# A graph layer on one core: float32 rows and sums in place of three bfloat16 parts, in-degrees per group of chunks, layernorm on whole pieces, no row loads

## The chip, the core and the metric

The kernel runs on one core of a Trainium2 chip. The metric is the device time of one execution in microseconds, lower being better. A core has five engines that work side by side and wait for one another by semaphores: PE (TensorE, matrix products into PSUM), DVE (VectorE, elementwise work and reductions), ACT (ScalarE, functions and copies), POOL (GpSimd, which here does nothing but issue the indirect DMAs that gather rows), and SP (SyncE, which issues plain DMAs). SBUF is the on-chip memory of 128 partitions; the table of node features is in DRAM.

## The reference

12,500 nodes with 128 features each, 200,000 edges sorted by destination, hidden width 512.

```python
h = relu(layernorm(x))                        # rows of 128, eps 1e-5
agg = segment_sum(h[src], dst, 12500)         # sum of h over a node's in-edges
deg = segment_sum(ones, dst, 12500)
agg = agg / maximum(deg, 1)
y = relu(agg @ Wg + h @ Ws + bg)              # 128 -> 128
y = tanh(y @ W1 + b1)                         # 128 -> 512
y = tanh(y @ W2 + b2)                         # 512 -> 512
out = x + y @ W3 + b3                         # 512 -> 128
```

All of it is float32.

## The kernel before

*Chunks.* The edges are cut into 1563 chunks of 128. Since the edges are sorted, the destinations of chunk c lie close to node 8c; each chunk has a window of 144 nodes around that place (88 or 56 for the last ones). A chunk is summed with a matrix product: the gathered rows, one edge on each partition, are the weights, and a 0/1 matrix `oh` (edge by window node, one where the edge's destination is that node) is the moving operand. The result, features by nodes, is added into the PSUM tile `agg` of the block to which the window's nodes belong. A block is 512 nodes (the last blocks are 256, three times 128 and 84; 28 blocks in all), so some 64 chunks belong to one; a window that lies across two blocks' border is done in two halves. A second product with a matrix of ones as weights adds the columns of `oh` into the PSUM tile `deg`: the in-degrees. Both are in `add(c)`; the call on PE itself is line 292.

*Rows in three parts.* `htab` in DRAM holds h as three bfloat16 numbers whose sum is the float32 number, 768 bytes a row (`split`, lines 175 to 178). So a chunk takes three bfloat16 products for `agg` and one for `deg`.

*Where rows come from.* Three kinds of chunks: 96 "raw" ones (12 groups of 8, one group in every 40 chunks from chunk 256 on) gather rows of x itself at the start (line 133), while h is still being made, and are normalized on their own later (`raw_parts`); 17 "slow" ones, one in every 80, have their 128 rows loaded one by one by SP (`row_loads`: SP reads an index into a register, line 323, and issues a DMA of one row, line 298); the other 1450 are gathered by POOL with one indirect DMA each (`gather`, line 302) into one of 28 row buffers (`AHEAD`). A gather whose buffer is not free waits for the products of the chunk that held it. SP also loads `xb`, a block's rows of x, and stores the output.

*Setup.* x comes in pieces of 14 tiles of 128 nodes (the first in two, 4 and 10). For each tile DVE computes `bn_stats` and `bn_aggr` (lines 159 and 160), for each piece `factors` gives scale and shift, ACT normalizes tile by tile (line 170), ACT and DVE split, and SP writes the piece to `htab` (line 221). Then the destinations are turned into places in their windows (`dloc`, line 242) and tested against the windows' ends (`bad`, line 254); the test decides at the end whether a general path has to run, which does not happen with these inputs.

*Order.* All PE work is in program order. The loop over chunks makes the one-hot matrices of a group of 8 chunks one group ahead (`onehot`, line 345, on DVE), issues gathers up to 28 ahead, adds the chunk, and when a block's last chunk is in, queues that block's `layers`. These are a generator of some 14 parts, one of which is issued after every second chunk: the reciprocal `rd` of the in-degrees on DVE (lines 438 and 439), `mT` = agg times rd (441), then on PE the products with Ws and Wg (`pm`, ACT makes h0, line 449), W1 (h1, line 455), W2 (16 products of 512 columns, h2, line 464), W3 (16 products into `pt`), and on DVE the sum with x and b3 (`o`, lines 475 and 478). `own(s)` loads a block's x 40 chunks before the next block begins and lets ACT normalize it again into `hb`; `own_turned` transposes it 30 chunks later. From chunk 1376 (`QUICK`) on, the parts are placed by an estimate `there` of when a chunk's rows land.

Of the kernel before, what the change touches and what calls it, by code (L numbers as in the profile page):

```python
"""Pre-LN graph layer: x + MLP(relu(mean_agg(h) @ Wg + h @ Ws + bg)), h = relu(layernorm(x)).

Edges are taken 128 at a time. The rows h[src] of a chunk come by an indirect DMA, as three bfloat16
parts whose sum is exactly the float32 row. A chunk's destinations are compared with a fixed window
of nodes around those it would have if the sorted destinations were spread evenly; the rows times
that 0/1 matrix add the chunk's part of the sums, transposed, to PSUM, and a matrix of ones times it
the in-degrees. Some groups of chunks, gathered while h is still being made, take rows of x and are
normalized on their own. One chunk in many has its rows loaded one by one, by the sync engine, at
addresses read from its indices, beside the indirect DMAs of the others. When all chunks that reach
a block of nodes are done, its layers follow.  # L10

Whether every destination lies in its chunk's window is checked on the chip. If one does not, a
general path, for edges in any order, computes everything anew.
"""
# [7 lines left out]
F32 = mybir.dt.float32  # L22
BF16 = mybir.dt.bfloat16
# [6 lines left out]
P = 128  # L30
EPS = 1e-5
CPR = 16       # chunks of edges in a row of the index tiles
BLK = 512      # nodes in a block
PIECE = 14     # tiles of nodes in a piece of x
GRP = 8        # chunks of edges in a group
NRAW = 12      # groups that take rows of x
RAW0 = 256     # first chunk of the first of those
STEP = 40      # chunks from one of those to the next
AHEAD = 28     # chunks whose rows are loaded ahead
SLOW0 = 160    # first of the chunks whose rows are loaded one by one  # L40
EACH = 80      # gathers from one of those to the next
LOADS = 16     # rows whose indices are read together
QUICK = 1376   # from this chunk on, the layers go ahead as soon as they can
# First chunks and windows' widths: the spread of the destinations about even ones falls to the end.
WINDOWS = ((0, 144), (1496, 88), (1536, 56))
W_RAW = 160    # width in the groups that take rows of x
W_MAX = max(W_RAW, *(w for _, w in WINDOWS))

# In the general path:
NCOPY = 4      # tables of sums, and chunks of edges in a group  # L50
GPIECE = 16    # tiles of nodes in a piece of x
GAHEAD = 3     # groups of edges whose rows are loaded ahead


def windowed(ctx, tc, x, src, dst, Wg, Ws, bg, W1, b1, W2, b2, W3, b3, out, flag):
# [5 lines left out]
    NT = -(-N // P)            # tiles of 128 nodes: node = 128 * tile + partition  # L61
    NP = NT * P
    ROW = CPR * P              # edges in a row of the index tiles
# [7 lines left out]
    per = N * P // E           # nodes that a chunk spans when all are even  # L71
# [3 lines left out]
    # The raw groups are those that take rows of x; an edge of one lies anywhere in its group.  # L75
# [3 lines left out]
    # The slow chunks are those whose rows are loaded one by one, by the sync engine, which has  # L79
    # little else to do.  # L80
    slow, n = [], 0
    for c in range(SLOW0, NCH - 1):
        n -= not raw(c)
        if n < 0 and not raw(c):
            slow.append(c)
            n = EACH

    # A window lies around the nodes that its chunk spans when all are even.
# [18 lines left out]
    rows_one = ctx.enter_context(tc.tile_pool(name="rows_one", bufs=3))  # L107
# [8 lines left out]
    rsrc = const.tile([P, NRAW, GRP], I32, name="rsrc")  # L116
    rdst = const.tile([P, NRAW, GRP], I32, name="rdst")
    for t, a in ((rsrc, src), (rdst, dst)):
        a = a[RAW0 * P : RAW1 * P].rearrange("(u e) -> u e", u=NRAW)[:, : GRP * P]
        nc.sync.dma_start(t, a.rearrange("u (p k) -> p u k", p=P))  # L120
# [21 lines left out]
    nc.vector.memset(ones, 1.0)  # L142
    eps = const.tile([P, 1], F32, name="eps")
    nc.vector.memset(eps, EPS)
    lane = ps_c.tile([P, W_MAX], F32, name="lane")
    nc.vector.tensor_copy(lane, lane_i)

# [1 line left out]
    htab = dram.tile([NP, 3 * D], BF16, name="htab")  # L149
    scol = const.tile([P, NCOL], I32, name="scol")  # L150
    dloc = const.tile([P, NCOL], F32, name="dloc")
    norm_x = const.tile([P, 2, NT], F32, name="norm_x")
    norm_raw = const.tile([P, 2, NRAW * GRP], F32, name="norm_raw")
    mv_raw = const.tile([P, NRAW * GRP, 2], F32, name="mv_raw")

    def moments(pool, mv, xt, k):
        st = pool.tile([P, PIECE, 6], F32, name="st")
        for t in range(k):
            nc.vector.bn_stats(st[:, t, :], xt[:, t, :])
            nc.vector.bn_aggr(mv[:, t, :], st[:, t, :])  # L160

    def factors(norm, mv):
        rstd, shift = norm[:, 0], norm[:, 1]
        nc.scalar.activation(rstd, mv[:, :, 1], AF.Sqrt, bias=eps)
        nc.vector.reciprocal(rstd, rstd)
        nc.vector.scalar_tensor_tensor(shift, mv[:, :, 0], -1.0, rstd, op0=ALU.mult, op1=ALU.mult)

    def normalize(h, xt, k, norm):
        for t in range(k):
            nc.scalar.activation(  # L170
                h[:, t, :], xt[:, t, :], AF.Relu, bias=norm[:, 1, t : t + 1], scale=norm[:, 0, t : t + 1]
            )

    def split(parts, h):
        nc.scalar.copy(parts[:, :, 0, :], h)
        nc.vector.tensor_tensor(h, h, parts[:, :, 0, :], op=ALU.subtract)
        nc.scalar.copy(parts[:, :, 1, :], h)
        nc.vector.tensor_tensor(parts[:, :, 2, :], h, parts[:, :, 1, :], op=ALU.subtract)

    with tc.tile_pool(name="setup", bufs=1) as sp, tc.tile_pool(name="ln", bufs=2) as ln:  # L180

        def indices(name, a, col, pad):
# [9 lines left out]
            # Column r * CPR + q is chunk q of row r, with an edge on each partition.  # L192
# [7 lines left out]
        # The first piece in two, so that the work on it begins early.  # L200
        pieces = [(0, 4), (4, PIECE - 4)] + [(t, min(PIECE, NT - t)) for t in range(PIECE, NT, PIECE)]
        for i, (t0, k) in enumerate(pieces):
# [8 lines left out]
            if i == 1:  # L211
                indices("src", src, scol, 0)
            norm = norm_x[:, :, t0 : t0 + k]
            mv = ln.tile([P, PIECE, 2], F32, name="mv")
            moments(ln, mv, xt, k)
            factors(norm, mv[:, :k])
            h = ln.tile([P, PIECE, D], F32, name="h")
            normalize(h, xt, k, norm)
            parts = ln.tile([P, PIECE, 3, D], BF16, name="parts")
            split(parts[:, :k], h[:, :k])  # L220
            nc.sync.dma_start(
                htab[t0 * P : (t0 + k) * P, :].rearrange("(t p) d -> p t d", p=P),
                parts[:, :k].rearrange("p t s d -> p t (s d)"),
            )

# [16 lines left out]
        nc.vector.tensor_tensor(dloc, dloc, low, op=ALU.subtract)  # L242
# [38 lines left out]
    nc.scalar.dma_start(b3r, bass.AP(tensor=b3.tensor, offset=b3.offset, ap=[[0, P], [1, D]]))  # L281

# [5 lines left out]
    class pe:  # L288
        """TensorE's instructions, in the order in which they are written here."""
# [10 lines left out]
    def gather(c):  # L300
        r = rows_in.tile([P, 3, D], BF16, name="rows")
        nc.gpsimd.indirect_dma_start(  # L302
            out=r.rearrange("p s d -> p (s d)"), out_offset=None, in_=htab,
            in_offset=bass.IndirectOffsetOnAxis(ap=scol[:, c : c + 1], axis=0),
        )
        rows_t[c] = r

    def indices_of(c):
        ix = ed.tile([1, P], I32, name="ix")
        sp_dma(ix, src[c * P : (c + 1) * P].rearrange("(o p) -> o p", o=1))  # L310
        return ix

    def row_loads():
        nxt_ix = indices_of(slow[0])
        for c in slow:
            ix = nxt_ix
            if c != slow[-1]:
                nxt_ix = indices_of(slow[slow.index(c) + 1])
            r = rows_one.tile([P, 3, D], BF16, name="srows")
            rows_t[c] = r  # L320
            rf = r.rearrange("p s d -> p (s d)")
            for p0 in range(0, P, LOADS):
                loads, at = nc.values_load_multi_w_load_instructions(  # L323
                    ix[:, p0 : p0 + LOADS], engines=[mybir.EngineType.SP], min_val=0, max_val=N - 1,
                    skip_runtime_bounds_check_because="src holds rows of x, as the indirect DMAs take it to",
                )
                for ld in loads:
                    tc.keep_in_program_order(ld)
                for p, v in enumerate(at, p0):
                    sp_dma(rf[p : p + 1, :], htab[bass.ds(v, 1), :])  # L330
                yield
# [587 lines left out]
```

## Time and profile before

| what | value |
|---|---|
| time, median of 3 runs | 2479.76 us (2448.73 to 2499.01) |
| span of the profiled execution | 2489.8 us, 32159 instructions |
| raw gathers (L133), first start to last end | 7.9 to 131.6 us |
| first gather from htab (L302) | 192.83 us |
| first chunk on PE | 200.37 us |
| last gather's start | 2445.80 us |
| last block: mT to end | 2475.26 to 2489.8 us |

The profile is of one execution. "Busy" is the time in which an engine executes; "idle before" is the engine's idle time ahead of a group of instructions, with what ended most of it: another engine's instruction, a DMA, "issue" (nothing that the profile shows), or "remote" (an event whose source is not known). A matmul of float32 is recorded as two. Two more lines of the page: the granted TensorE clock in 40 equal slices of the span, in tenths of full speed, and the group of the degree products.

```profile
PEclk9996566766876787677767668578577577576688
L292 PE MATMUL deg<-oh,ones 128*128 128x144 bf16 (+21 forms) x2010 | 476.6, 247 | 159.4 <-issue 158.7
```

The number in the middle of such a line (247 ns) is an instruction's own length from start to modelled end. Matmuls overlap, so it is not the distance from one to the next.

### The profile page before, as it was taken

The page shows a single profiled execution, that of the slowest core. Times are in us where ns is not written, and L with a number is a line of the kernel's source. Part 1 is how long each engine was busy: PE and PEld are TensorE (multiplying, and loading weights), DVE is VectorE, ACT ScalarE, POOL GpSimd, SP SyncE. Part 2 cuts the span into 40 slices and gives each one's busy share as a digit, 9 for nine tenths or more (in the row PEclk, how much of TensorE's full clock was granted, in tenths as well). Part 3 has the DMA queues.
Part 4 walks back from the last instruction along what each step waited for, and adds up shares of the span by engine and source line. Part 5 has one row for each costly group of instructions (what it writes and reads, how often), then busy time and mean ns, then how long its engine had stood idle before and what let it go on. Part 6 is the DMA issues. An engine that isn't in the chain of part 4 may idle for free. (4 is left out here: it accounts for less than half of the span.)

```text
span 2489.8 us, 32159 instructions
## 1 busy us (share of the span) xinstructions
PE 1408.8 (57%) x10187; PEld 927.2 (37%) x10187; DVE 549.9 (22%) x935; ACT 335.9 (13%) x620; POOL 1480.4 (59%) x1553
## 2 busy tenths in 40 slices
PE   0002465656774676567656556567467466566568
PEld 0001233434453444344433334334334343343437
DVE  3162331121322122212211112111111211112111
ACT  2160025100110111011001001001001010010012
POOL 6706665665656555665666666656656665666661
PEclk9996566766876787677767668578577577576688
DMA  5353222222222222222222222222222222222221
GB/s 138 81 171 92 72 71 69 73 71 67 75 65 67 65 68 61 71 72 65 70 70 74 70 72 75 68 70 76 71 67 68 74 76 68 69 80 71 72 72 30
DMA packets 135478, 185.45 MB, mean 74 GB/s; under 512 B 32669, under 2 KB 109726, under 8 KB 135104
## 3 DMA queue, kind: packets, MB, share of 16 engines
q0 software_dynamic: 72672, 148.93, 22.4%
q1 hardware_dynamic: 59466, 31.00, 4.5%
q10 hardware_dynamic: 3160, 3.38, 0.5%
q8 instruction: 82, 1.34, 0.2%
q14 instruction: 98, 0.80, 0.1%
HBM read 167.16 MB, written 16.03 MB: 74 GB/s over the span
## 5 line engine op out<-in xcount | busy, mean ns | idle before, releaser
L302 POOL DMA_INDIRECT rows<-htab,scol x1450 | 1384.8, 955 | 930.3 <-issue 321.3
L292 PE MATMUL agg<-oh,rows 128*128 128x144 bf16 (+16 forms) x5574 | 649.7, 246 | 437.8 <-issue 423.4
L292 PEld LDWEIGHTS <-rows 128*128 128x128 bf16 x5574 | 479.2, 116 | 688.8 <-issue 673.2
L345 DVE TENSOR_TENSOR oh<-lane,dloc 128x1152 bf16<-128x1152 f32 (+3 forms) x196 | 261.4, 1334 | 1592.3 <-remote 640.9
L292 PE MATMUL pm<-h,w 128*128 128x512 f32 (+3 forms) x1120 | 516.0, 595 | 96.3 <-issue 36.8
L292 PE MATMUL deg<-oh,ones 128*128 128x144 bf16 (+21 forms) x2010 | 476.6, 247 | 159.4 <-issue 158.7
L292 PEld LDWEIGHTS pm<-h,w 128*128 128x128 f32 x1120 | 202.1, 207 | 251.9 <-issue 179.4
L292 PEld LDWEIGHTS <-ones 128*128 128x128 bf16 x2010 | 233.3, 116 | 159.7 <-issue 159.2
L292 PE MATMUL pm<-mT,wg 128*128 128x512 f32 (+3 forms) x56 | 48.6, 967 | 120.2 <-DVE mT L441 64.2
L133 POOL DMA_INDIRECT raw<-in_x_dram,rsrc x96 | 94.8, 987 | 35.4 <-issue 29.0
L464 ACT ACTIVATE h<-pm,b2c 128x512 f32<-128x512 f32 (+3 forms) x112 | 70.4, 632 | 324.0 <-PE pm L292 183.4
L449 ACT ACTIVATE h<-pm,bgc 128x512 f32<-128x512 f32 (+3 forms) x28 | 17.7, 633 | 710.3 <-PE pm L292 288.0
L197 PE MATMUL pm<-ident,idx_f 98*128 98x98 f32 x32 | 6.5, 378 | 180.6 <-DVE idx_f L191 175.2
L292 PE MATMUL pt<-w,h 128*128 128x128 f32 (+1 forms) x784 | 96.0, 278 | 5.0 <-issue 2.5
L455 ACT ACTIVATE h<-pm,b1c 128x512 f32<-128x512 f32 (+3 forms) x112 | 68.7, 632 | 205.0 <-remote 96.6
L292 PEld LDWEIGHTS pt<-w,h 128*128 128x128 f32 (+1 forms) x784 | 90.5, 191 | 7.3 <-issue 4.2
L403 ACT COPY hT<-pt 128x512 f32<-128x512 f32 (+1 forms) x25 | 14.4, 578 | 564.7 <-PE agg L292 301.7
L439 DVE RECIPROCAL rd<-rd 128x512 f32<-128x512 f32 (+3 forms) x28 | 82.4, 2941 | 0.8
L197 PEld LDWEIGHTS pm<-ident,idx_f 98*128 98x128 f32 x32 | 5.0, 222 | 181.8 <-issue 157.6
L292 PEld LDWEIGHTS pm<-mT,wg 128*128 128x128 f32 x56 | 12.8, 282 | 149.0 <-DVE mT L441 78.1
L292 PE MATMUL agg<-oh,rparts 128*128 128x160 bf16 (+2 forms) x384 | 47.6, 256 | 24.7 <-issue 24.5
L292 PEld LDWEIGHTS <-rparts 128*128 128x128 bf16 x384 | 34.3, 119 | 43.5 <-issue 43.3
(66 smaller groups left out, 530.5 us busy)
## 6 DMA issues: line engine op xcount, KB each, us to landing
srows<-htab SPq DMA_DIRECT2D x2176, 0.8 KB
rows<-htab,scol POOLq DMA_INDIRECT x1450
htab<-parts SPq DMA_DIRECT2D x6, 1344.0 KB
xb<-in_x_dram SPq DMA_DIRECT2D x24, 256.0 KB
out_dram<-o SPq DMA_DIRECT2D x23, 256.0 KB
xt<-in_x_dram SPq DMA_DIRECT2D x5, 896.0 KB
raw<-in_x_dram,rsrc POOLq DMA_INDIRECT x96
w<-in_L_gnn_W_dram ACTq DMA_DIRECT2D x1, 1024.0 KB
```

Source lines behind the costliest of these rows:

```text
L133: nc.gpsimd.indirect_dma_start(out=t[:, j, :], out_offset=None, in_=x, in_offset=bass.IndirectOffsetOnAxis(ap=rsrc[:, g, j : j + 1], axis=0),)
L197: nc.tensor.transpose(p[:, q, :NROW], rf[:, (q0 + q) * P : (q0 + q + 1) * P], ident[:NROW, :NROW])
L292: tc.keep_in_program_order(nc.tensor.matmul(*a, **k))
L302: nc.gpsimd.indirect_dma_start(out=r.rearrange("p s d -> p (s d)"), out_offset=None, in_=htab, in_offset=bass.IndirectOffsetOnAxis(ap=scol ...
L345: nc.vector.tensor_tensor(oh[:, :k, :w], lane[:, None, :w].to_broadcast([P, k, w]), dloc[:, g * GRP : g * GRP + k][:, :, None].to_broadcas ...
L403: nc.scalar.copy(hT[:, : k * P], pt[:, :k, :].rearrange("p t n -> p (t n)"))
L439: nc.vector.reciprocal(rd[:, :n], rd[:, :n])
L449: nc.scalar.activation(h0[:, :n], p0[:, :n], AF.Relu, bias=bgc)
L455: nc.scalar.activation(h1[:, m, :n], p1[:, :n], AF.Tanh, bias=b1c[:, m : m + 1])
L464: nc.scalar.activation(h2[:, m, :n], p2[:, :n], AF.Tanh, bias=b2c[:, m : m + 1])
```

## The change

1. `htab` holds float32 rows of 512 bytes; a chunk is one float32 product into `agg`. `split` and the three parts go.
2. The one-hot matrices are float32, in three fixed buffers `oh0` to `oh2` of pitch 200, zeroed once; raw groups have their own, `ohr`.
3. In-degrees: for each group of 8 chunks whose windows are evenly spaced, DVE adds up the group's one-hot matrices along the nodes with one strided `tensor_reduce` into `cnt` (bfloat16), and one bfloat16 product with the ones adds it to `deg` in the middle of the group before. Groups at the changes of window width take a float32 product per chunk. `rd` is computed as soon as a block's last group is counted.
4. Layernorm works on a whole piece: a reduce for the mean, a `scalar_tensor_tensor` that centres, an ACT Square, a reduce, Sqrt and reciprocal, and a `scalar_tensor_tensor` that takes the maximum with 0 and scales. The statistics lie in PSUM. Raw groups do the same (`centre` in groups 2 to 13, `raw_scaled` in the group ahead).
5. The slow chunks, their row loads and index loads are gone; all 1467 chunks that are not raw are gathered by POOL.
6. `own` loads hb from `htab` by a DMA in place of normalizing x on ACT. b3 and the node numbers `lane` share a PSUM tile; `dloc` is made in parts of 512 columns by way of PSUM.
7. The raw indices are loaded in two DMAs each, group 0 first. The estimate `there` has other constants.

```diff
-    rows_one = ctx.enter_context(tc.tile_pool(name="rows_one", bufs=3))
...
-        nc.sync.dma_start(t, a.rearrange("u (p k) -> p u k", p=P))
+        for u0, u1 in ((0, 1), (1, NRAW)):
+            nc.sync.dma_start(t[:, u0:u1], a[u0:u1].rearrange("u (p k) -> p u k", p=P))
...
-    htab = dram.tile([NP, 3 * D], BF16, name="htab")
+    htab = dram.tile([NP, D], F32, name="htab")
...
+    def centre(pool, xt, k, stats):
+        nc.vector.tensor_reduce(stats[:, 0], xt, AX.X, ALU.add)
+        nc.vector.scalar_tensor_tensor(xt, spread(stats[:, 0], k), -1.0 / D, xt, op0=ALU.mult, op1=ALU.add)
+        sq = pool.tile([P, k, D], F32, name=f"sq{k}")
+        nc.scalar.activation(sq, xt, AF.Square)
+        nc.vector.tensor_reduce(stats[:, 1], sq, AX.X, ALU.add)
+    def factors(stats):
+        nc.scalar.activation(stats[:, 1], stats[:, 1], AF.Sqrt, bias=eps, scale=1.0 / D)
+        nc.vector.reciprocal(stats[:, 1], stats[:, 1])
+    def scale(h, xt, k, stats):
+        nc.vector.scalar_tensor_tensor(h, xt, 0.0, spread(stats[:, 1], k), op0=ALU.max, op1=ALU.mult)
...
-        r = rows_in.tile([P, 3, D], BF16, name="rows")
+        r = rows_in.tile([P, D], F32, name="rows")
...
-    def row_loads():
...
+    PITCH = WINDOWS[0][1] + per * (GRP - 1)
+    oh_bufs = [const.tile([P, GRP, PITCH], F32, name=f"oh{i}") for i in range(3)]
...
-        oh = ed.tile([P, GRP, W_MAX], BF16, name="oh")
+        oh = ed.tile([P, GRP, W_RAW], F32, name="ohr", bufs=2) if is_raw else oh_bufs[g % 3]
...
+            cnt = ed.tile([P, PITCH], BF16, name="cnt")
+            part, row, col = oh.ap
+            shifted = bass.AP(tensor=oh.tensor, offset=oh.offset, ap=[part, [col[0], n], [step * col[0], k]])
+                nc.vector.tensor_reduce(cnt[:, :n], shifted, AX.X, ALU.add)
...
-            for s in range(3):
-                pe.matmul(
-                    ag[:, a0 - n : a1 - n], parts[:, s, :], rhs, start=first and s == 0, stop=last and s == 2,
-                    skip_group_check=True,
-                )
-            pe.matmul(dg[:, a0 - n : a1 - n], ones, rhs, start=first, stop=last, skip_group_check=True)
+            pe.matmul(
+                acc[b][:, a0 - n : a1 - n], rows, oh[:, a0 - lo : a1 - lo], start=first, stop=last,
+                skip_group_check=True,
+            )
...
-        hb = ml.tile([P, BLK // P, D], F32, name="hb", bufs=1)
-        normalize(hb, xb, k, norm_x[:, :, n0 // P : n0 // P + k])
+        hb = ml.tile([P, BLK // P, D], F32, name="hb")
+        sp_dma(hb[:, :k], htab[n0 : n0 + k * P, :].rearrange("(t p) d -> p t d", p=P))
...
+        if c % GRP == GRP // 2 and g + 1 < ngrp:
+            count(g + 1)
...
-            there = 5.5 + 1.04 * (NRAW * GRP + order.index(c)) if c not in slow else 0
+            there = 12.0 + 1.25 * (NRAW * GRP + order.index(c))
```

## The prediction

> **What bounds the kernel now.** I read the page's groups first, then the list of waits, then the timelines of POOL, PE and SP around one block, then windows with and without row loads.
>
> ```profile
> PE 1408.8 (57%) x10187; PEld 927.2 (37%) x10187; DVE 549.9 (22%) x935; ACT 335.9 (13%) x620; POOL 1480.4 (59%) x1553
> L302 POOL DMA_INDIRECT rows<-htab,scol x1450 | 1384.8, 955 | 930.3 <-issue 321.3
> L292 PE MATMUL agg<-oh,rows 128*128 128x144 bf16 (+16 forms) x5574 | 649.7, 246 | 437.8 <-issue 423.4
> srows<-htab SPq DMA_DIRECT2D x2176, 0.8 KB
> ```
>
> No engine is full. POOL issues a gather in 0.955 us and idles 930 us between gathers. The waits say on whom:
>
> ```profile
> PE agg L292 <- issue: 456.5, 613, 2.6
> PE agg L292 <- DMA rows<-htab,scol: 8.4, 10, 1.2
> POOL rows L302 <- PE agg L292: 240.5, 189, 8.6
> POOL rows L302 <- remote: 203.6, 165, 5.1
> POOL rows L302 <- DVE bad L254: 61.2, 1, 61.2
> ```
>
> PE waits 8.4 us in all for rows, POOL hundreds for PE to free a row buffer (28 of them). So PE is late, and what it waits for is "issue": nothing that the profile shows. The timelines of SP and PE, columns start, length, instruction, count, idle before:
>
> ```profile
> 1537.92 0.41 SPq L298 DMA_DIRECT2D out_dram<-o  x1
> 1540.42 24.00 SPq L298 DMA_DIRECT2D srows<-htab  x23
> ```
> ```profile
> 1541.00 0.35 PE L292 MATMUL agg<-oh,rows 128*128 128x144 bf16 x3
> 1541.19 0.23 PE L292 MATMUL deg<-oh,ones 128*128 128x144 bf16 x1
> 1541.93 0.22 PE L292 MATMUL agg<-oh,rows 128*128 128x144 bf16 x1 [0.52 <-issue]
> 1542.67 0.22 PE L292 MATMUL agg<-oh,rows 128*128 128x144 bf16 x1 [0.52 <-issue]
> 1543.40 0.22 PE L292 MATMUL agg<-oh,rows 128*128 128x144 bf16 x1 [0.51 <-issue]
> ```
>
> While SP rests, PE does a chunk of four matmuls in 0.25 us; 1.5 us after SP resumes its one-row loads, PE does one matmul in 0.74. I counted PE's gaps of over 0.6 us that no wait explains: 865 (719 us) in the 1965 us with row loads, 15 to 18 (12 to 14 us) in 385 us without. The windows behind the last row load (2361) and before it, columns length, then busy time of PE, PE's loads, DVE, ACT, POOL, then clock, DMA share, GB/s:
>
> ```profile
> 2310.00:2360.00 50.00, 25.63 (x242) 20.15 (x241) 6.26 (x6) 2.81 (x6) 31.90 (x34) 0.65 0.27 73
> 2364.00:2415.00 51.00, 38.70 (x276) 21.82 (x274) 10.66 (x10) 6.19 (x9) 32.44 (x35) 0.87 0.26 68
> ```
>
> POOL, when it isn't held up, and at the start:
>
> ```profile
> 130.69 0.95 POOL L133 DMA_INDIRECT raw<-in_x_dram,rsrc  x1 [0.30 <-issue]
> 192.83 0.95 POOL L302 DMA_INDIRECT rows<-htab,scol  x1 [61.20 <-DVE bad L254]
> 194.08 0.94 POOL L302 DMA_INDIRECT rows<-htab,scol  x1 [0.30 <-issue]
> ```
>
> A free gather comes every 1.25 us (1.2526 over the 78% of gathers that don't wait), with 512 B rows of x (L133) and 768 B rows of htab (L302) alike. The 1450 gathers run from 192.83 to 2445.80: 2253 us, where 1450×1.2526 = 1816 would do. Excess 437 us, caused by PE.
>
> **The change part by part.** The sum follows POOL.
>
> *Start.* Raw gathers start at 7.9 us, once all raw indices are in. The change loads group 0's indices by DMAs of their own (two more on SP, ahead of x's first piece); I take 4 us, bounds 3.5 (nothing else on that path) and 8. 96 gathers at their present mean of 1.29 are 124 us: raw ends at 128 (now 131.6).
>
> *The 61 us gap* is htab being late: per tile, bn_stats, bn_aggr, then the split, on DVE, whose dependent small operations come 2.4 to 2.8 us apart while raw gathers run and 0.2 apart afterwards. The change has four whole passes per piece of 14 tiles: two reduces and two scalar_tensor_tensors. By the rows "144.24 2.01 DVE L176" (1792 elements) and "192.01 0.94 DVE L254 TENSOR_REDUCE" (760, so 2.1 for 1792), a piece is 8.2 us; with two hand-overs to ACT and back at 2.5 us delay, 13.8. Seven pieces' worth: 57 to 97 us, plus some 25 for loads, indices and the last store: 85 to 120 us, at worst 165 if every pass is delayed twice. Mostly under 128, so the gap goes; bounds 0 to 40 us, I take 0. What is late next is POOL itself.
>
> *Row loads gone, 17 chunks more by gather.* SP loses 2176 one-row DMAs and 17 index loads, and gains 25 loads of htab (own's hb, 256 KB) in place of 98 ACT normalizes; each is issued some 30 chunks (37 us) before PE transposes it, so nothing waits. 1467 gathers × 1.2526 = 1838 us: last gather at 128 + 1838 = 1966.
>
> *End.* Before, the last gather is 44 us from the end since PE is behind. With PE up to date: landing 2.7 us (gather 201.60, PE uses it 204.34), the last block from mT 2475.26 to the end 2489.8 = 14.5 us, its last chunks 3: 20 us, giving 1986.
>
> *Can PE keep up?* A chunk is now one f32 matmul in place of four bf16 ones (0.25 us at full clock). Nearest rows: "1533.38 3.78 PE L292 MATMUL pt<-w,h 128*128 128x128 f32 x32" is 16 f32 matmuls with a new weight each, 0.236; four 512-column f32 matmuls take 3.65, by columns 0.257 for 144. I take 0.26. A block of 512 nodes: about 46 whole and 36 split chunk matmuls (a window that crosses a block's edge) 46×0.26 + 36×0.236 = 20.5, eight or nine degree matmuls 0.7, layers 24.5 as now (22×0.91, 16×0.236, 4 transposes): 46 us at full clock, 65 at a granted 0.7, 91 at half. POOL brings a block in 64×1.2526 = 80 us (64 us where 13 of 64 chunks are raw). The layers' parts are spread over some 28 chunks (35 us), where PE owes 32 at full clock, so it falls behind by perhaps 12 to 20 us; 28 buffers hold 35. Allowance for POOL held up: 10 us (0 to 60).
>
> A rule speaks against this. The row: PE's weight load took 116 ns for bf16 rows and 191 ns for f32 (pt<-w,h). The Trainium skill, "TensorE: Matmul & The Clock Gate", section "Weight-path perf modes — Fast Weight Load (FWL) and DoubleRow", says that the fast load path is off for FP32 weights, and rows are the weights here. If nothing of it were hidden, a chunk costs two loads and two half passes, 2×(191+60) = 0.5 us, and a block 82×0.5 + 25 = 66 us, still under 80; by the x32 row, where the same loads run, it is 46. I take the row; the rule's value is in the range through the half clock.
>
> *VectorE.* One-hot to f32: 1.36 us now per group of 8, same element count. New: cnt, a strided reduce of 1600 elements, 1.9 us by the 760-element row; rd as now. About 8×3.3 + 6 = 32 us of 80 per block; in groups 2 to 13 the raw centring adds 3.3 of 10 us. The new wait: PE's degree matmul of group g+1 stands before chunk 5 of group g, with all later chunk matmuls queued behind it. Its cnt is begun at chunk 0, so 3.3 us of work has 5 us of cover; if that is lost, PE slips within the buffers' 35 us. The fixed oh buffers are three as before; the b3 and lane reads from PSUM, the zeroing and the copies around dloc lie in the shade of raw gathers or at 0.1 us; none touches POOL.
>
> *Sum:* 1986 + 10 = 1996 us of span against 2489.8. The profiled execution lies 0.4% above the median 2479.76 (runs 2448.73 to 2499.01): 1996×0.996 = **1990 us**.
>
> **The rivals.**
>
> *PE still late (2040 to 2490, centre 2130).* The 0.7 us gaps may come from POOL's gathers as well, or PE may sit at half clock. For: 11 of the 15 gaps without row loads lie behind 2361, where only gathers run; DVE is also delayed while raw gathers run and SP is still. Also the clock in chunk stretches is 0.58 to 0.72, and PE will be idler. Against: 2364–2415 has 38.7 of 51 us busy at 0.87. At half clock throughout, 91 us per block × 24.4 blocks + 60 of ends = 2280; if PE lost 35% of its time as now, 65 us grew to 100 a block, 2490 after scaling: no change; with a fourth of the chunk instructions, and so fewer gaps, some 85 a block: 2130.
>
> *DVE blocks the gathers (slower).* If each group's 3.3 us of one-hot and cnt stopped POOL for its whole length, a gather took 1.2526 + 0.41 = 1.66, and 128 + 1467×1.66 + 20 = 2583, ×0.996 = 2573. It passes "before" from an interval of 1.60 on. For: the Trainium skill, "SBUF — State Buffer", section "Who interferes with whom", gives DVE instructions with two SBUF inputs, and 2-port modes, an exclusive lock against GpSimd; the new centring and scaling are of two inputs (why stats sit in PSUM). Against, in the trace:
>
> ```profile
> 1515.49 1.36 DVE L345 TENSOR_TENSOR oh<-lane,dloc 128x1152 bf16<-128x1152 f32 x1 [13.55 <-PE deg L292]
> ```
> ```profile
> 1514.96 0.95 POOL L302 DMA_INDIRECT rows<-htab,scol  x1 [0.30 <-issue]
> 1516.21 0.94 POOL L302 DMA_INDIRECT rows<-htab,scol  x1 [0.30 <-issue]
> 1517.46 0.95 POOL L302 DMA_INDIRECT rows<-htab,scol  x1 [0.30 <-issue]
> ```
>
> The one-hot overlaps two gathers and neither is longer; the same section says that tensor_reduce never contends on trn2, which no row here shows for a strided one.
>
> **How the numbers follow.** POOL sets the time, 1960 to 2040: 0.72. PE still late: 0.19, and 0.04 more for its far end near no change. DVE blocks POOL: 0.05. About 2% is what a measurement of this kernel can tell from none: faster 0.91, same 0.04, slower 0.05. Low end 1955: the sum without allowance (1986×0.996 = 1978), less the 1.2% by which the fastest run before lies under the median. High end 2130: a gap of 40, 60 held up by PE, and the nearer half of the first rival.
>
> **What would show it.** Right: rows<-htab one every 1.25 us with 0.30 idle from about 128 us on; PE's waits end on "DMA rows" instead of issue; no runs of 0.7 us gaps; agg f32 matmuls near 0.26 apart; cnt near 1.9 us; the last gather near 1966. Wrong: POOL still waiting for PE agg (PE late), gathers or their gaps growing beside L336's reduce (DVE blocks), or a wait of tens of us before the first rows gather (htab late).

## The result, and the profile after

The changed kernel took 2388.21 us (median of 4 runs, 2376.89 to 2401.97) against 2476.83 us (4 runs, 2448.73 to 2499.01) of the kernel before: a ratio of 0.970, with an interval of 0.962 to 0.979. It is faster by 3%, where 20% was forecast. (Ratios here and below leave out slow runs, those over 1.5% above the fastest of their kernel, so they differ a little from the quotients of the medians, here 0.964.) The profiled execution has a span of 2384.5 us.

The page of the changed kernel, in the rows that answer to those shown of before:

```profile
PE 1389.0 (58%) x6517; PEld 1058.9 (44%) x6517; DVE 1079.8 (45%) x777; ACT 208.6 (9%) x316; POOL 1482.0 (62%) x1570
L290 POOL DMA_INDIRECT rows<-htab,scol x1467 | 1387.5, 946 | 822.8 <-issue 296.7
L280 PE MATMUL agg<-oh,rows 128*128 128x144 f32 (+17 forms) x3764 | 707.9, 331 | 296.3 <-issue 288.2
```

and its list of waits (engine, what waits, for what: us in all, times, longest):

```profile
PE agg L280 <- issue: 326.1, 301, 2.6
POOL rows L290 <- PE agg L280: 265.6, 258, 16.8
POOL rows L290 <- remote: 188.6, 158, 4.6
```

SP's one-row loads are gone, a chunk is one product instead of four, and the picture is the same: POOL idles 823 us between gathers, much of it for row buffers that PE has not freed, and PE stands still for "issue". One such place, on PE, DVE and POOL (start, length, instruction, idle before):

```profile
1461.01 0.77 PE L280 MATMUL agg<-oh,rows 128*128 128x44 f32 x3 [1.52 <-issue]
1489.09 0.35 PE L280 MATMUL deg<-cnt,ones 128*128 128x4 bf16 x2 [27.32 <-issue]
```
```profile
1454.63 1.34 DVE L324 TENSOR_TENSOR oh<-shared,dloc 128x1152 f32<-128x1152 f32 x1
1484.93 1.36 DVE L324 TENSOR_TENSOR oh<-shared,dloc 128x1152 f32<-128x1152 f32 x1 [28.96 <-remote]
```
```profile
1480.21 0.95 POOL L290 DMA_INDIRECT rows<-htab,scol  x1 [0.30 <-issue]
1485.17 0.95 POOL L290 DMA_INDIRECT rows<-htab,scol  x1 [4.02 <-remote]
```

PE's products up to 1461 have freed a one-hot buffer and row buffers. DVE, which needs the one, and POOL, which needs the others, both go on only at 1485: the news reached them some 23 us late, and PE's degree product in turn waits for DVE's `cnt`. In the trace's record of semaphore updates, most of PE's come within some 15 ns of a product's end up to 1449.3; from then on, while POOL issues 25 gathers one after the other, they trickle in, four of them 1.45 us apart and the rest at 1459.6, 1470.2, 1479.3 and 1484.9. Taken over the whole run (for each product that updates a semaphore, the time from its modelled end to PE's next recorded update, by how many gathers had followed each other without a pause): the median is 14 ns after up to two gathers, some 0.4 us after three to five, 0.7 to 1.1 us after six to ten (it depends on which pauses count) and 2.2 us beyond. The kernel before shows the same rise: 0.3 to 0.7, some 1.2, 2 to 2.5 and some 3.2 us. DVE's and ACT's updates are late too, in after over 1 us in 228 of DVE's 601 and 78 of ACT's 290. So the lateness on this core goes with gathers in a row. It is more than late updates: in the kernel before, about 500 of some 800 gaps between PE's starts lie between two products of which neither updates a semaphore (as those at 1541.93 and 1542.67 in the prediction's rows). So PE's own starts are held up as well.

Whether a core is held up in this way is no property of the two kernels. In the experiments the kernel before, on one core, ran in 1991 to 1997 us in the groups of E1 to E4, E5 to E7, E11 to E14 and E18 (the runs of a group were made together, on one chip), and in 2457 to 2481 us, as on the record, in E8 to E10 and E15 to E17; one chip showed both. The two kinds are called free and held-up cores below, and a free core is compared with free ones alone, a held-up one with held-up ones.

### The profile page after: what moved, and what is told of

Its sections match the earlier page's. It is cut to its first block, busy times and chain, and to the rows that moved or that the text cites. A ratio compares the mean times of both kernels' runs of the same rounds, so it can differ in the third digit from the quotient of the medians.

```text
span 2384.5 us, 17685 instructions
## 1 busy us (share of the span) xinstructions
PE 1389.0 (58%) x6517; PEld 1058.9 (44%) x6517; DVE 1079.8 (45%) x777; ACT 208.6 (9%) x316; POOL 1482.0 (62%) x1570
## 4 chain that ended last, share of the span: by engine, by line
PE 36%; another core or an unknown queue 35%; issue 13%; DVE 12%; ACT 2%; DMA 1%; POOL 0%; SPq 0%; DVEq 0%; ACTq 0%; POOLq 0%
PE pm L280 19%; PE agg L280 13%; DVE cnt L336 4%; DVE oh L324 3%; PE pt L280 3%; PE deg L280 1%; DVE rd L381 1%; DMA xt<-in_x_dram 1%; ACT h L473 1%; POOL rows L290 0%; DVE raw L154 0%; DVE h L164 0%; ACT h L467 0%; DVE xt L154 0%
## 5 line engine op out<-in xcount | busy, mean ns | idle before, releaser
L280 PE MATMUL agg<-oh,rows 128*128 128x144 f32 (+17 forms) x3764 | 707.9, 331 | 296.3 <-issue 288.2
L280 PEld LDWEIGHTS agg<-oh,rows 128*128 128x128 f32 x3764 | 666.9, 243 | 476.7 <-issue 464.9
L324 DVE TENSOR_TENSOR oh<-shared,dloc 128x1152 f32<-128x1152 f32 (+1 forms) x184 | 247.2, 1350 | 968.2 <-remote 536.2
L336 DVE TENSOR_REDUCE cnt<-oh 128x200 bf16<-128x1600 f32 (+1 forms) x180 | 508.2, 2841 | 3.9 <-DVE flag L247 1.0
L280 PE MATMUL deg<-cnt,ones 128*128 128x200 bf16 (+9 forms) x290 | 55.9, 246 | 227.9 <-issue 149.6
L280 PEld LDWEIGHTS <-ones 128*128 128x128 bf16 x290 | 34.9, 123 | 187.0 <-issue 186.2
L280 PE MATMUL agg<-ohr,raw 128*128 128x160 f32 (+2 forms) x256 | 53.5, 341 | 38.1 <-issue 38.0
L280 PEld LDWEIGHTS agg<-ohr,raw 128*128 128x128 f32 x256 | 49.1, 246 | 50.2 <-issue 49.5
L493 DVE TENSOR_TENSOR o<-pt,xb 128x512 f32<-128x512 f32 x23 | 15.9, 690 | 90.1 <-PE pt L280 84.2
L380 DVE TENSOR_SCALAR rd<-deg 128x512 f32<-128x512 f32 (+3 forms) x28 | 17.3, 618 | 66.8 <-PE agg L280 33.8
```

The costliest lines, as they stand in the source:

```text
L280: tc.keep_in_program_order(nc.tensor.matmul(*a, **k))
L324: nc.vector.tensor_tensor(oh[:, :k, :wide], lane[:, None, :wide].to_broadcast([P, k, wide]), dloc[:, g * GRP : g * GRP + k][:, :, None].to ...
L336: nc.vector.tensor_reduce(cnt[:, :n], shifted, AX.X, ALU.add)
L380: nc.vector.tensor_scalar(rd[:, :m], dg[:, :m], 1.0, None, op0=ALU.max)
L493: nc.vector.tensor_tensor(o[:, :whole], po[:, :whole], xb[:, :whole], op=ALU.add)
```

## The experiments

Theory 0 is the prediction's: SP's one-row loads make PE's gaps. Theory 1: POOL's gathers do. Theory 2: PE's gaps are its own.

**E1 to E4.** A probe, and three edits. In the probe, PE multiplies a tile and DVE copies the product back into it: one such turn needs an update from each to the other, so a late update makes a long turn. The turn, and the gathers that run beside it:

```python
kp(nc.tensor.matmul(pp, lhs, ball, start=True, stop=True))
kp(nc.vector.tensor_copy(ball, pp))
...
kp(nc.gpsimd.indirect_dma_start(
    out=rows[i], out_offset=None, in_=x,
    in_offset=bass.IndirectOffsetOnAxis(ap=ix[:, i : i + 1], axis=0),
))
```

E2 takes the slow chunks out of the kernel before (a guard for the empty list is left out here):

```diff
-        if n < 0 and not raw(c):
+        if False:
             slow.append(c)
...
```

E3 puts a pause on POOL behind every gather of the changed kernel, and E4 takes row buffers by four (seven of four chunks each, freed together):

```diff
+        tc.keep_in_program_order(nc.gpsimd.iota(lane_i, pattern=[[1, W_MAX]], base=0, channel_multiplier=0))
```
```diff
-        r = rows_in.tile([P, D], F32, name="rows")
+        if i % 4 == 0:
+            quads[0] = rows_in.tile([P, 4, D], F32, name="rows")
+        r = quads[0][:, i % 4, :]
...
```

> A probe, not the layer: PE and DVE hand a tile to and fro 48 times (matmul, copy from PSUM), alone (A), beside 32 gathers issued one after the other (B), beside 32 iotas on POOL of about 1 us (C), beside gathers with an iota of about 0.3 us (D) or about 1 us (E) after each, beside 32 one-row loads by SP (F); then 96 matmuls each read by DVE, alone (G) and beside gathers (H). Theory 1 (gathers one after the other hold up the semaphore updates of the other engines): a turn takes under 1 us in A, C and F and 2 us or more in B, less in D and E than in B; H takes at least twice G. Theory 2 (PE's gaps are PE's own: its loads, its clock): all of A to F within 10%, H as G. Theory 0 (the prediction's: SP's one-row loads): only F is slow.

> The kernel before without its 17 slow chunks; POOL gathers those too. Theory 0: PE's gaps without a wait go, POOL sets the time: 193 + 1467 x 1.2526 + 25 = 2056 us. Theory 1: the gaps stay, since the gathers stay; 17 more gathers and less traffic by SP, 2380 to 2480 us. Theory 2: 2440 to 2500 us.

> The changed kernel with an iota of 0.25 us on POOL behind each gather from htab, so that gathers come no closer than 1.5 us. Theory 1: PE's semaphore updates are prompt again, PE keeps up, and the time is POOL's: 128 + 1467 x 1.5 + 20 = 2350 us, no slower than the changed kernel although POOL has 370 us more to do. Theory 2: PE is as late as ever and POOL's share is added in part: 2390 to 2600 us.

> The changed kernel with seven row buffers of four chunks each in place of 28 of one: a buffer is free when the fourth product has read it, so only every fourth gather waits for PE. Theory 1: the update that POOL needs is one in four, POOL runs on for four gathers and PE is held up as before or more; between 2250 and 2400 us. Theory 2: no change, 2370 to 2410 us. If the cushion of 28 buffers is what counts, slower by 1 to 3%, since up to three free chunks wait for the fourth.

The kernel before took 1996.5 us here (7 runs): free cores, on which no theory of a hold-up can be tested. E1: 0.527 us a turn in all of A to F, 0.467 us a matmul in G and H. E2: 2018.45 us, ratio 1.0109 (1.0092 to 1.0126): 17 gathers more at 1.25 us are 21 us, and 22 were measured. E3: 2219.41 us, ratio 1.112; gathers came every 1.413 us, not 1.5, since POOL idles 0.16 us between an iota and a gather, where it idles 0.30 between two gathers. POOL alone sets the time: 127 + 1467 × 1.413 + 19 = 2219. E4: 1987.75 us, ratio 0.9945 (0.9927 to 0.9963), where E5 will be; buffers by four change nothing on a free core.

**E5 to E7.** Both kernels as they are, and the probe again.

> The changed kernel as it is, beside the kernel before on the same chip. The chip of the runs E1 to E4 ran the kernel before in 1996 us, that of the record in 2477; E4, nearly this kernel, took 1988. If what held PE up belongs to a chip and not to the two kernels: where the kernel before takes about 2000, this takes 1975 to 1995 (ratio 0.99 to 1.0), POOL gathering one chunk every 1.25 us; where it takes about 2480, 2377 to 2402 as on the record. If the change itself brings the hold-up, the ratio is above 1.1 on the quicker chip.

> The kernel before as it is, for its profile on this chip. Where it takes about 2000: PE waits for rows, gaps of 0.7 us without a wait are absent although SP issues its 2176 one-row loads; where it takes about 2480, as in the profile of before. Theory 0 (row loads make the gaps on any chip) wants the gaps in both.

> The probe of E1 again. Where the kernel before takes about 2000: 0.53 us a turn in all of A to F as in E1. Where it takes about 2480 theory 1 expects 0.53 in A and C and over 1 us in B, less in D and E.

Free cores again. The changed kernel took 1984.92 us against 1993.73, ratio 0.995 (0.9931 to 0.9968); the probe showed 0.53 us throughout. The page of E5, the changed kernel:

```profile
span 1985.8 us, 17685 instructions
L290 POOL DMA_INDIRECT rows<-htab,scol x1467 | 1387.2, 946 | 447.2 <-issue 207.3
L280 PE MATMUL agg<-oh,rows 128*128 128x144 f32 (+17 forms) x3764 | 945.2, 386 | 276.8 <-DMA rows<-htab,scol 265.7
```

and the page of E6, the kernel before:

```profile
span 1993.5 us, 32159 instructions
L302 POOL DMA_INDIRECT rows<-htab,scol x1450 | 1383.8, 954 | 442.2 <-issue 325.4
L292 PE MATMUL agg<-oh,rows 128*128 128x144 bf16 (+16 forms) x5574 | 624.8, 248 | 526.4 <-DMA rows<-htab,scol 523.8
srows<-htab SPq DMA_DIRECT2D x2176, 0.8 KB
```

In both, PE's products wait for rows and for next to nothing else; POOL's 0.30 us between gathers is all its idle time. E6 has every one-row load that the profile of before has. Gaps (starts over 0.6 us apart within the chunks' products, with no wait on the later one) are some 800 to 900 in before and 360 to 440 in after, by how a wait is told, but 15 in E6 and 10 in E5. PE's updates come 14 ns after the product in the median of E5, though nearly all of its gathers follow each other without a pause, and never over 0.24 us. Theory 0 falls: with all the row loads there and the gaps absent, the row loads do not make them by themselves. Theory 2 falls too, since the same PE work runs without gaps; nor do gathers in a row make them everywhere, for POOL gathers as fast here: only some cores show them.

**E8 to E10.** The changed kernel with the 17 slow chunks put back (`row_loads` as before, rows of 512 B, and `sq` in two buffers), the probe under load, and the changed kernel on eight cores.

```diff
-    order = [c for c in range(NCH) if not raw(c)]
+    order = [c for c in range(NCH) if not raw(c) and c not in slow]
+    loading = row_loads()
...
```
```diff
-    r = _run(nc, [arrays], core_ids=[0])
+    r = _run(nc, [arrays] * 8, core_ids=list(range(8)))
```

> The changed kernel with the 17 slow chunks back, their float32 rows of 512 B loaded one by one by SP as before. Where nothing holds PE up, POOL sets the time and has 17 gathers less: 1985 - 17 x 1.25 = 1964 us, ratio to the kernel before 0.984, the fastest of all. Theory 0 (one-row loads hold PE up): above 2050 us. On a chip that takes 2480 for the kernel before: 2380 to 2450.

> The probe with more load of the core's own: turns of PE and DVE alone (A), beside gathers (B), beside gathers with 48 one-row loads by SP and 48 by ACT (C), beside gathers with 16 loads of 512 KB by SP and ACT (D), and a stream of 96 matmuls beside all of C's loads (E). If the hold-up of the record comes from the traffic of transfers or of their completions on the core, a turn rises from 0.53 to over 0.7 us in C or D, or E shows gaps of 0.7 us. If it belongs to the other chip or to what else ran there: 0.53 throughout, E as before at 0.47 a matmul.

> The changed kernel, the same program on all eight cores of the chip at once, each with its own copy of the inputs; the time is that of the slowest core. If a busy neighbour is what holds up PE's semaphore updates: 2300 us or more, late updates behind six and more gathers in a row, as in the profile of after. If not: 1980 to 2050 us, updates prompt.

Held-up cores now, on the chip of E5 to E7; the kernel before took 2480.93 us. E8: 2419.45 us, ratio 0.983 (0.976 to 0.990). E9's turns: 0.527 us alone (A); means of 0.96 beside gathers (B), 0.98 with the one-row loads (C), 0.90 with the large loads (D); the stream E took 0.73 a matmul, against 0.47 in E1. So gathers alone do it. What the core's own loads add is small and not settled by one stage each: the 32 gathers of a stage cost the turns 20 us in B, 28 in C and 23 in D (all of the time over 0.527 us a turn). PE in B of E9, 18 us after its first gather:

```profile
69.12 0.21 PE L78 MATMUL pp<-ball,lhs 128*128 128x64 bf16 x1 [0.31 <-DVE ball L79]
69.65 0.21 PE L78 MATMUL pp<-ball,lhs 128*128 128x64 bf16 x1 [0.32 <-DVE ball L79]
71.96 0.21 PE L78 MATMUL pp<-ball,lhs 128*128 128x64 bf16 x1 [2.10 <-issue]
74.80 0.21 PE L78 MATMUL pp<-ball,lhs 128*128 128x64 bf16 x1 [1.90 <-DVE ball L79]
```

(One turn of 0.73 lies between the last two rows.) The turns are even until 15 gathers have gone out, then they break up. E10 shows both kinds of core in one execution, by die:

```profile
core 0: 2417.6 us, clock 0.736
core 1: 2496.9 us, clock 0.726
core 2: 2383.8 us, clock 0.741
core 3: 2488.2 us, clock 0.728
core 4: 1977.2 us, clock 0.754
core 5: 1928.0 us, clock 0.759
core 6: 1978.3 us, clock 0.750
core 7: 1931.4 us, clock 0.758
```

All eight run the same program, so a busy neighbour alone is not enough: cores 4 to 7 have busy neighbours too.

**E11 to E14.** Four kernels on eight cores, to see both kinds at once: before (E11), E2's (E12), E3's (E13), E8's (E14).

> The kernel before on all eight cores. If both kinds of cores are there as in E10 (2384 to 2497 and 1928 to 1978 us): before takes 2450 to 2600 on the held-up ones and 1935 to 1995 on the others, that is 0 to 1% above E10 core by core there. If no core is held up: 1935 to 2000 on all.

> The kernel before without one-row loads, on all eight cores. On the held-up cores theory 0 (row loads make the gaps) gives about 2060, theory 1 (the gathers) 2400 to 2600, near E11. On the others, 17 gathers more than E11: 21 us above it core by core.

> The changed kernel with a pause behind each gather (E3: one gather every 1.41 us, 2217 us), on all eight cores. On the held-up cores theory 1, in its strong form, says that the pause lets the semaphore updates through, so they come near the others: 2200 to 2300, faster than E10 there although POOL has more to do. If the number of gathers counts and not their pace, or if the cause lies elsewhere: 2400 to 2650. On the others 2150 to 2220.

> The changed kernel with the 17 slow chunks loaded by SP (E8), on all eight cores. On cores that nothing holds up: 17 gathers fewer than E10, 21 us less core by core (1907 to 1957), the fastest of all. On held-up cores as E10, 2380 to 2600; if row loads add to the hold-up, 3% more or worse.

In each, one die was held up and one free; the kinds hold the same cores within a group (cores 4 to 7 were held up here), and the kernel before, alone on core 0, was each time of the kind of its die. Means over the four cores of a kind and the executions given (three each, one for E13), in us:

| kernel | free cores | held-up cores | held-up, per gather |
|---|---|---|---|
| E11 before | 1964 (1936 to 1996) | 2542 (2478 to 2633) | 1.64 |
| E12 before, no row loads | 1989 (1960 to 2018) | 2607 (2473 to 2720) | 1.67 |
| E10 after | 1961 (1923 to 2038) | 2498 (2368 to 2668) | 1.60 |
| E13 after, pause | 2252 (2216 to 2311) | 2507 (2367 to 2658) | 1.60 |
| E14 after, row loads | 1934 (1905 to 1962) | 2505 (2408 to 2648) | 1.62 |

(The last column is the mean divided by all gathers, 1546 or 1563.) On held-up cores, taking the row loads out does not bring 2060 us, and the pause does not bring 2217: theory 0 falls there as well, and so does the strong form of theory 1. What stays nearly equal is the time per gather. On free cores everything follows the number of gathers: E12 is 24 us above E11, E14 28 us below E10.

**E15 to E17.** The probe at several paces (an iota of so many columns behind each gather), on eight cores; E8's kernel and the changed one side by side.

```python
gathers(fresh()); rally(120)
gathers(fresh(), 192); rally(135)
gathers(fresh(), 600); rally(170)
gathers(fresh(), 1024); rally(200)
gathers(fresh(), 0, 64); rally(120)
```

> The probe of E1 on eight cores, each stage with 48 gathers and more turns: alone (A), gathers at 1.25 us (B), 1.42 us (C), about 1.75 us (D) and 2.1 us (E) from one to the next, gathers of 64 rows one after the other (F), 48 plain loads of 128 rows by SP (G). The profile is of the slowest, held-up core. If each gather brings about 1.55 us of something that the other engines' semaphore updates queue behind: turns of 0.53 us in A, D, E and G, well above in B (mean 0.9 or more in the second half of the gathers), less above in C. If gathers at any pace do it: D and E slow too. If it is transfers of any kind: G slow too. F is slow as B if the count of gathers matters, quick if their rows do.

> The changed kernel with row loads, on one core. Where the kernel before takes about 1995: 1964 us, ratio 0.985, below E17. Where it takes about 2480: 2400 to 2430, within 2% of E17.

> The changed kernel itself beside E16. Where the kernel before takes about 1995: 1985 us; where it takes about 2480: 2377 to 2402.

E15 on core 3, held up, and on core 4, free, of one execution; windows in stage B, columns length, busy time and instructions of PE, its loads, DVE and POOL, clock, DMA share, GB/s:

```profile
40.00:50.00 10.00, 4.02 (x19) 1.99 (x19) 4.26 (x20) 7.70 (x8) 1.00 0.18 47
50.00:60.00 10.00, 1.27 (x6) 0.63 (x6) 1.20 (x6) 7.75 (x9) 1.00 0.21 52
60.00:97.00 37.00, 2.20 (x11) 1.13 (x11) 2.47 (x11) 28.91 (x31) 1.00 0.22 55
100.00:145.00 45.00, 11.43 (x54) 5.67 (x54) 12.34 (x55) 0.00 (x0) 1.00 0.00 0
```
```profile
40.00:50.00 10.00, 4.02 (x19) 1.98 (x19) 4.26 (x20) 7.63 (x8) 1.00 0.19 47
50.00:60.00 10.00, 4.02 (x19) 1.99 (x19) 4.27 (x20) 7.56 (x9) 1.00 0.20 52
60.00:97.00 37.00, 14.81 (x70) 7.31 (x70) 15.84 (x71) 27.85 (x31) 1.00 0.20 52
```

POOL issues 31 gathers in the 37 us on both; PE makes 11 turns where the free core makes 70. The granted clock is 1.00 throughout, so it is not the clock. By pace, on the held-up cores 0 to 3: one gather in 1.25 us (1.21 on cores 1 and 3) breaks the turns up from gather 9 to 15 on; in 1.42 us from 24 on (core 3), 26 (core 1), 48 (core 2), or not at all (core 0); in 1.76 and 2.1 us never. Gathers of 64 rows (1.17 to 1.21 us apart) do it from gather 10 to 13 on, and 48 plain loads of 128 rows by SP never. So it is the number of gathers per time that counts, not their rows and not transfers as such; whether a plain DMA issued by POOL does it too was not run.

It is as if each gather left something that takes longer to clear than the gather takes to issue, and the other engines queue behind it. If on core 3 the same backlog is reached after 9 gathers at 1.214 us and after 24 at 1.42, then 9 × (s − 1.214) = 24 × (s − 1.42), and s is 1.54 us; core 1 (12 and 26) gives 1.60, core 2 (11 at 1.25, 48) 1.47. These are estimates, but two things bear them out. The turns stay broken up after the last gather, on core 3 until 120 us though POOL was done at 98 (last line of its windows: 54 turns in 45 us, where 85 fit at 0.527); from the first gather to the last long turn it is 1.41 to 1.67 us for each of the 48 gathers, by core. And on the record, from the first to the last gather of htab, it is 1.507 us each in after, and 1.498 in E17. POOL may go ahead of that until the row buffers are used up, and then has to wait; that would be why the pace of E3 gains nothing on such a core (E13). The delays come in steps: most long turns on core 0 take 2.1 or 2.8 us and on core 1 2.2 or 2.9, three and four times some 0.7, and PE's lone products in the prediction's rows lie 0.74 apart. What is served in such steps, no run shows.

On a held-up core in one group, E16 took 2411.12 us (2401 to 2427; ratio 0.984, 0.973 to 0.994) and E17 2369.39 us (2359 to 2378; ratio 0.967, 0.956 to 0.978). The changed kernel is the quicker of the two there, though it has 17 gathers more; with row loads a gather came every 1.549 us (E8: 1.550; before: 1.555), without every 1.498.

**E18.** E2's kernel once more, for the held-up case.

> The kernel before without one-row loads (E2), on one core. On a held-up core (the kernel before at 2430 to 2500): if row loads cost 0.05 us per gather, 193 + 1467 x 1.50 + 45 = 2440, ratio 0.985; if they cost nothing, 17 gathers more at 1.55, 2500, ratio 1.01; theory 0, all of the excess, 2056. On a free core as E2: 2018, ratio 1.011.

A free core: 2014.51 us against 1991.46, ratio 1.012 (1.010 to 1.014), as E2. What row loads cost the kernel before on a held-up core stays open: E16 and E17 speak for some 40 to 70 us, E11 and E12 for nothing.

## Why the prediction was wrong, point by point

Predicted, measured on the record, and on free cores (E6 to E5), as changes in us:

| term | predicted | record | free cores |
|---|---|---|---|
| first gather from htab | -65 (192.8 to 128) | -65 (to 127.7) | -21 (148.8 to 127.7) |
| first to last gather | -415 (2253 to 1838) | -44 (to 2209) | +8 (1825 to 1833) |
| last gather to the end | -24 (44 to 20) | +4 (47.7) | +5 (20.0 to 25.0) |
| allowance | +10 | none | none |
| span | -494 | -105 | -8 |

**The step that failed** is "Excess 437 us, caused by PE", with the count of gaps that put PE's lateness down to the row loads: 865 gaps with them, 15 to 18 without. The count can stand; the inference was wrong. Row loads and gathers fall into the same stretches, namely those of plain chunks: in the 20 pauses of SP of over 4 us (359 us), PE starts 2.8 products of the layers per us, beside row loads 0.4, so the stretches without row loads were those in which PE had other work. What the runs showed in its place: with all 2176 row loads there and a free core (E6) the gaps and the excess are gone, and on a held-up core gathers alone delay PE, DVE and ACT (E9's stage B, E15), at some 1.5 us for each gather. The window behind the last row load that was shown, 2364 to 2415, held 11 of the gaps in question, with gathers running and SP still: that was the row to believe, and it was used for the rival alone. On the record the excess over 1.2526 us per gather fell from 437 to 372 us, not to 0.

**The first rival**, that the gaps come with the gathers themselves, was right in its cause and had a chance of 0.19. Its sum of 2130 let the lateness shrink with PE's instructions; it is set by gathers, of which there are 17 more. Its far end, 2490, was nearer.

**What held.** On a free core, the size of the other terms: raw gathers from 4.6 to 127.4 us (4 and 128 predicted), no gap before htab's first row, one gather every 1.2504 us on a free core (1.2526), a chunk's product, on the record, 0.249 us at full clock (eight chunks from 1445.01 to the next product at 1447.00; 0.26 predicted). On the record the start did not hold as a whole: gathers from htab began at 127.7, but PE's first chunk came at 162.3 (130.2 in E5), and POOL, out of row buffers, stood still from 162.4 to 179.3. On free cores the forecast of 1990 us for the changed kernel meets E5's 1985; there the kernel before already takes 1994. So the sum described the changed kernel without hold-up, and compared it with a kernel before that was held up.

**The fast weight load** of the Trainium skill's "TensorE: Matmul & The Clock Gate", section "Weight-path perf modes — Fast Weight Load (FWL) and DoubleRow", is off for FP32 weights, and the trace agrees: the loads of float32 rows took 243 ns on the record against 116 in bfloat16, but beside the products, which stayed at 0.249 us a chunk. The row was the right choice for whole chunks. A chunk split between two blocks took 0.45 us (five of them from 1451.90 to 1454.2, clock 1.00), though it has the same 144 columns: there the load was not hidden, and the 0.236 that the prediction took for each part is near.

**The start gap** of 61 us was DVE's small operations 2.4 us apart, taken for a fact of the old layernorm. It is the hold-up again: on a free core (E6) the first gather from htab starts 1.3 us after the last raw one. That the change removes it on a held-up core because it has few dependent steps is likely, but no run shows it by itself.

**cnt** was mis-sized, 1.9 us for the strided reduce of 1600 elements, 2.84 measured, with the price off the path on a free core (PE waits 10.7 us in all for it in E5; 78 on the record, where DVE itself starts late). **The slower rival** did not come: gathers from htab took 0.946 us each, and in E5 the 439 that start during the strided reduce of `cnt` took 0.946 as well, like those that start while DVE rests. That answers what no row of before could show of a strided reduce.

Left open: what the updates and PE's starts queue behind, why it strikes the cores of one die at one time and not at another, and whether recording the profile has a part in it. The last is a rival that nothing here rules out: every run has its span and clock from such a recording, so none was made without it.

The fastest kernel differs by core: on free ones E14, the changed kernel with row loads (28 us below E10 on average, though on another chip and die); on held-up ones the changed kernel itself (E17).

## What to carry to other kernels

Before a stall that no wait explains is priced to a suspect, look for stretches with one suspect and without the other; two things that always run together cannot be told apart by counting. Run the kernel before once more, elsewhere, before pricing a stall that is more than 10% of it: here the excess was absent on free cores. Where POOL's gathers set the pace, count gathers, not bytes or rows, and, as advice that no run here tests by itself, keep the other engines' dependent steps few.

## What the runs showed of the hardware

Gathers in a row can hold up the semaphore updates of PE, DVE and ACT, and PE's starts, by 1 to some 20 us, on all cores of one die at some times and not at others: at one gather per 1.21 to 1.25 us after a run-up of 9 to 15 gathers, at 1.42 us on three cores of four and after 24 or more, at 1.76 us never (E15).

A gather of 64 rows is issued nearly as slowly as one of 128 (1.17 to 1.21 us from one to the next against 1.21 to 1.25, core by core in E15): most of the cost is the instruction's, not the rows'.

On a free core the old layernorm lengthens raw gathers. POOL and DVE in E6, the kernel before:

```profile
62.47 0.95 POOL L133 DMA_INDIRECT raw<-in_x_dram,rsrc  x1 [0.30 <-issue]
63.72 2.22 POOL L133 DMA_INDIRECT raw<-in_x_dram,rsrc  x1 [0.30 <-issue]
```
```profile
63.10 2.03 DVE L178 TENSOR_TENSOR parts<-h,parts 128x1792 bf16<-128x1792 f32 x1 [0.59 <-ACT parts L177]
65.04 0.48 DVE L159 BATCH_NORM_STATS2 st<-xt 128x6 f32<-128x128 f32 x2
```

The gather that starts during L178's subtraction of two SBUF tiles takes 2.22 us. The 13 that start during such a subtraction (L176, L178) take 2.07 us on average, the 46 that start while DVE rests 0.95. Over the 96 raw gathers that is 111.6 us in E6 against 93.9 in E5, which keeps one operand of such steps in PSUM: 18 of the 21 us by which E5's first gather from htab comes earlier. The Trainium skill, "SBUF — State Buffer", "Who interferes with whom", says that a DVE instruction with two SBUF inputs contends with a GpSimd instruction that reads SBUF; the gathers read their indices there, and here a run agrees.
